# Nine row gathers move from GpSimd to single-row loads on SyncE and ScalarE, in a recurrent scoring kernel

## The chip, the core and the metric

The kernel runs on one core of a Trainium2 chip. The metric is the device time of one execution in microseconds. Three runs before the change gave 1564.42, 1565.53 and 1565.64 us; the median is 1565.53 us. Engines are named as the profile names them: PE is TensorE, DVE is VectorE, ACT is ScalarE, POOL is GpSimd, SP is SyncE.

## What is computed

A batch of 1024 sequences of 50 item numbers looks up a table of 100001 rows of 128 floats. The running mean of the rows is normalised over the batch, drives a neuron that spikes, and the mean spike count of each sequence is multiplied with the whole table.

```python
emb = emb_table.at[0].set(0.0)
e = emb[seq]                              # 1024 x 50 x 128
prefix = jnp.cumsum(e, axis=1)
uF = prefix / jnp.minimum(t_idx, lengths)
y = (uF - uF.mean(axis=0)) * lax.rsqrt(uF.var(axis=0) + BN_EPS) * gamma + beta
def step(v, x):                           # scanned over the 50 steps
    v = v + (x - v) / TAU
    spike = atan_spike(v - V_TH)
    return v - spike * V_TH, spike
scores = spikes.mean(axis=0) @ emb.T      # 1024 x 100001
```

The scores take 409.6 MB in HBM; they are the kernel's output.

## The kernel before

**Two stages.** The first runs the 50 steps. The second multiplies the counts with the table in 98 parts of 1024 rows (L498 to L578): PE multiplies (L161), DVE and ACT move the product from PSUM to SBUF (L553, L555), and SP issues the stores (L170). The table's first parts are loaded at the very start of the kernel (L110), over some 60 us.

**One step.** The batch is eight pieces of 128 sequences. For step t, `gather(t)` (L205) makes a tile `e` of 128 x 1024, and POOL issues one indirect load for each piece (L208). There are two buffers of `e`, so the gathers of step t+2 stand behind PE's last reading of the `e` of step t. PE turns the eight pieces one after the other into `pre` (L351), which keeps the running sum, in two halves of four. For each half DVE scales the sum into `uF` (L362) and takes statistics (L363). Then follow in turn: DVE's aggregate (L371), ACT's square root (L375) and centring of `uF` (L382), small steps on DVE (L388 to L401), ACT's `x` (L405), DVE's step that makes the new `v` (L408), and ACT's `over` (L321), which makes the tile `d` from `v`. `d` is used in the next step. `uF` has one buffer and `pre` is one sum, so two steps overlap little on PE, DVE and ACT; only the gathers run ahead, by two buffers.

**The single rows.** In six steps (`BY_SYNC`, L36) the eighth piece is not gathered. `fetch_singles` (L221) has SP load the byte addresses of 16 rows into registers (L226, a TENSOR_LOAD) and issue 16 loads of one row of 512 bytes (L229), eight times over. The 128 rows land in one of four slots of `held_rows`, and PE reads the slot as its eighth piece (L353). The first set is written into the program ahead of the steps, each further set in the step that uses up the set before. SP has nothing else to do in the first stage after the loads of the table.

**What holds a load back.** All loads and stores of SP and ACT take turns on eight counting semaphores, DMAHW0 to DMAHW7, in an order that is fixed when the program is built. A load adds 16 to its semaphore when its data has landed, and waits, on the engine that issues it, until the load before it on the same semaphore has landed. In the first stage before the change only SP issues such loads.

Of the kernel before, what the change touches and what calls it, by code (L numbers as in the profile page):

```python
# [17 lines left out]
U8 = mybir.dt.uint8  # L18
# [3 lines left out]
P = 128  # L22
# [4 lines left out]
BANK = 512  # L27
# [5 lines left out]
SHIFT = TWICE + ASIDE  # L33
FURTHER = {5: 1, 6: 2}

BY_SYNC = (12, 19, 26, 33, 40, 47)  # L36
AT_ONCE = 16

WIDTHS = 4 * [2] + 4 * [3] + 13 * [6]
NARROW, MIDDLE = 4, 8  # L40
# [3 lines left out]
def rec_kernel(  # L44
# [9 lines left out]
    nc = tc.nc  # L54
    B, T = seq.shape
    N, D = table.shape
    NB = B // P
# [16 lines left out]
    held_rows = const.tile([P, BANK], F32, tag="countB", name="held_rows")  # L74
# [13 lines left out]
    def pair(i):  # L88
        free.append([embp.tile([P, HALF], F32R, tag=f"{x}{i}", name=f"{x}_{i}") for x in ("hi", "lo")])
# [59 lines left out]
    def prepare(q, pt):  # L149
        turned(q, pt)  # L150
        split[q] = hi, lo = free.pop(0)
        vp, vh, vl = views(q, pt, hi, lo)
        nc.scalar.copy(vh, vp)  # L153
        nc.vector.tensor_tensor(vl, vp, vh.bitcast(F32), ALU.subtract)  # L154
# [18 lines left out]
    with ExitStack() as ph:  # L173
# [30 lines left out]

        def gather(t):  # L205
            es[t] = gp.tile([P, B], F32, tag="e", name=f"e_{t}")
            for n in range(NB - (t in BY_SYNC)):
                nc.gpsimd.indirect_dma_start(  # L208
                    out=es[t][:, n * P : (n + 1) * P],
                    out_offset=None,  # L210
                    in_=table,
                    in_offset=bass.IndirectOffsetOnAxis(ap=idx[:, n, t : t + 1].bitcast(U32), axis=0),
                )

        byte_rows = table.rearrange("n d -> (n d)").bitcast(U8)
        row_bytes = 4 * D
        starts = ids[:T, :P].bitcast(I32)
        regs = [nc.sync.alloc_register(f"row{k}") for k in range(AT_ONCE)]
        singles = {}

        def fetch_singles(i):  # L221
            t = BY_SYNC[i]
            rows_of = held_rows[:, i % (BANK // P) * P :][:, :P]
            singles[t] = rows_of
            for p0 in range(0, P, AT_ONCE):
                nc.sync.load(regs, starts[t : t + 1, p0 : p0 + AT_ONCE])  # L226
                for k, reg in enumerate(regs):
                    at = nc.sync.snap(reg, donate=True, min_val=0, max_val=(N - 1) * row_bytes)
                    nc.sync.dma_start(  # L229
                        out=rows_of[p0 + k : p0 + k + 1, :].bitcast(U8),  # L230
                        in_=byte_rows[bass.ds(at, row_bytes)].rearrange("(o b) -> o b", o=1),
                    )

        make_identity(nc, ident)
        isz = up.tile([P, NB, P], F32, tag="uF", name="isz")
        rb = up.tile([P, NB, P], F32, tag="uF", name="rb")
        gather(0)

        last_ids = ids[:, P : P + T]
        nc.vector.tensor_copy(last_ids, idx[:, NB - 1, :])  # L240
        ips = vp.tile([P, B], F32, tag="v0", name="ips")
        nc.tensor.transpose(ips[:T, :P], last_ids, ident)
        nc.vector.tensor_scalar_mul(starts, ips[:T, :P], float(row_bytes))
        fetch_singles(0)

        nc.vector.memset(isz, 0.0)
# [47 lines left out]
        def only(t):  # L294

            k = t % ONLY
            if k == 0:
                n = min(ONLY, T - t)
                nc.vector.tensor_tensor(
                    ls[:, :n, :],  # L300
                    r0n.unsqueeze(1).to_broadcast([P, n, D]),
                    sel[:, t : t + n].unsqueeze(2).to_broadcast([P, n, D]),
                    ALU.mult,
                )
            return ls[:, k, :]
# [12 lines left out]
        def over(t, v):  # L318

            d = lp.tile([P, B], BF16, tag="d", name=f"d_{t}")  # L320
            nc.scalar.activation(d, v, AF.Identity, bias=less)  # L321
            return d
# [4 lines left out]
        def spiked(out, cs, v):  # L327
            nc.vector.scalar_tensor_tensor(out, v, V_TH, count[:, cs], ALU.is_ge, ALU.add)
# [12 lines left out]
        correct(0, only(0))  # L341
        l = only(1)
        gather(1)
        for t in range(T):
            last = t == T - 1
# [18 lines left out]
            if t + 2 < T:  # L364
                gather(t + 2)
            if t in BY_SYNC[:-1]:
                fetch_singles(BY_SYNC.index(t) + 1)
            if not last:
# [35 lines left out]
            def x(vt, cs):  # L404
                nc.scalar.activation(vt, uF[:, cs], AF.Identity, bias=hgb[:, 1:2], scale=a)  # L405

            def step(vt, cs):
                nc.vector.scalar_tensor_tensor(vt, negv[:, cs], -0.5, vt, ALU.mult, ALU.add)  # L408

            if not last:  # L410
                vt = vp.tile([P, B], F32, tag=f"v{(t + 1) % 2}", name=f"v_{t}")
                x(vt, whole)
                if t:
                    spiked(count, whole, v)
                step(vt, whole)
                v = vt
                if t == T - 2:
                    spiked(count, whole, v)
                    moved = once.tile([P, P], F32, tag="r0hi", name="moved")
                    nc.vector.tensor_scalar_add(moved, v[:, pieceA], beta2)  # L420
                    near = once.tile([P, P], F32, tag="r0", name="near")
                    nc.vector.scalar_tensor_tensor(near, v[:, pieceA], V_TH, moved, ALU.is_ge, ALU.subtract)
                d = over(t, v)
                if t + 2 < T:
                    l = only(t + 2)

                if t in (T - 8, T - 6):
                    q = (t - T + 8) // 2
                    pair(q)
                    prepare(q, vp.tile([P, HALF], F32, tag="v0", name=f"pt_{q}"))  # L430
                    if q == TWICE - 1:
                        for k in range(TWICE):
                            rows[GROUP + ASIDE + k] = first[:, k, :]
                        nc.sync.dma_start(
                            out=first[:, :TWICE, :],
                            in_=table[(GROUP + ASIDE) * HALF : (GROUP + SHIFT) * HALF, :].rearrange(
                                "(q p k) d -> p q (k d)", p=P, k=KQ
                            ),
                        )
# [58 lines left out]
    for c, W in enumerate(WIDTHS):  # L498
# [38 lines left out]
        for n, q in blockwise:  # L537
# [4 lines left out]
            o = os[n]  # L542
# [27 lines left out]
            if n in (1, 4) and c >= MIDDLE and to_fetch < parts:  # L570
                g, k = divmod(to_fetch - SHIFT, GROUP)
# [26 lines left out]
```

## Time and profile before

| | |
|---|---|
| median of three runs (lowest, highest) | 1565.53 us (1564.42, 1565.64) |
| profiled execution: its time, its span | 1564.15 us, 1562.4 us |
| first stage: first gather, last gather issued | 3.54 us, 496.29 us |
| first store of scores issued | 504.70 us |
| busy over the span: PE, DVE, ACT, POOL | 1118.9, 948.1, 673.4, 374.5 us |
| written to HBM | 409.60 MB |

The profile is one execution. Times in it count from the start of the span. Time is cut by engine, and each group of instructions has its line in the kernel, the tile it writes and reads, the count, the busy time and the idle time ahead of it with what ended that. Rows marked SPq or ACTq are loads issued by SP or ACT.

### The profile page before, as it was taken

What the parts mean: (1) busy time and instruction counts of PE and PEld (TensorE: products, weight loads), DVE (VectorE), ACT (ScalarE), POOL (GpSimd) and SP (SyncE); (2) the same over time, 40 slices, a digit from 0 to 9 for tenths busy, and PEclk for the clock granted to TensorE, in tenths of its full rate; (3) what the DMA queues carried; (4) which work ended last, traced back from release to release, by engine and by line L of the source; (5) the groups of instructions that cost most, each with busy time, mean ns of one, the idle gap of its engine ahead of it and who ended that gap; (6) DMA issues with size and microseconds to landing.
All of it is one profiled execution on the core that took longest, in us unless ns stands there. A gap on an engine that the chain in (4) does not pass through costs nothing.

```text
span 1562.4 us, 13860 instructions
## 1 busy us (share of the span) xinstructions
PE 1118.9 (72%) x4465; PEld 794.4 (51%) x4465; DVE 948.1 (61%) x1128; ACT 673.4 (43%) x698; POOL 374.5 (24%) x400
## 2 busy tenths in 40 slices
PE   4444444444445989989888888888877888877883
PEld 2212111111123767667666666666666666666663
DVE  5777677777778655667555555555555455555552
ACT  2333333333334545555444444444444444444442
POOL 7777777777775000000000000000000000000000
PEclk9999999999999999999999999999999899999998
DMA  9722222222222999999999999999999999999997
GB/s 347 269 54 54 55 55 54 54 55 54 52 80 62 402 411 416 421 414 396 431 422 429 433 425 406 432 424 432 416 425 421 402 428 425 429 422 418 430 409 338
DMA packets 52813, 488.22 MB, mean 312 GB/s; under 512 B 10767, under 2 KB 11792, under 8 KB 31620
## 3 DMA queue, kind: packets, MB, share of 16 engines
q1 hardware_dynamic: 32432, 431.26, 65.7%
q0 software_dynamic: 12608, 25.85, 6.3%
q10 hardware_dynamic: 7700, 30.23, 4.7%
q8 instruction: 35, 0.57, 0.1%
q14 instruction: 38, 0.31, 0.1%
HBM read 77.69 MB, written 409.60 MB: 312 GB/s over the span
## 4 chain that ended last, share of the span: by engine, by line
DMA 47%; POOL 19%; PE 13%; issue 10%; DVE 5%; ACT 4%; ACTq 0%; POOLq 0%; SPq 0%; DVEq 0%
DMA scores<-o 45%; POOL e L208 19%; PE po L161 13%; DVE o L553 3%; ACT o L555 3%; DMA e<-in_L_rec_emb_table,idx 3%; DVE pairs L154 1%; ACT pairs L153 0%; PE pt L137 0%; PE pre L351 0%; ACT hi L153 0%; PE warm L337 0%; DMA idx<-in_r_seq 0%; DVE lo L154 0%; ACTq L555 0%
## 5 line engine op out<-in xcount | busy, mean ns | idle before, releaser
L553 DVE TENSOR_SCALAR o<-po 128x1024 f32<-128x1024 f32 (+1 forms) x390 | 465.5, 1213 | 326.2 <-DMA scores<-o 192.1
L555 ACT ACTIVATE o<-po 128x1024 f32<-128x1024 f32 x392 | 392.6, 1026 | 498.4 <-DMA scores<-o 377.8
L208 POOL DMA_INDIRECT e<-in_L_rec_emb_table,idx x394 | 373.8, 949 | 122.1 <-issue 117.1
L161 PE MATMUL po<-pairs,countB 128*128 128x512 f32 (+1 forms) x1120 | 293.3, 408 | 65.3 <-ACT o L555 65.3
L351 PE MATMUL pre<-ident,e 128*128 128x128 f32 x394 | 174.9, 463 | 220.7 <-DMA e<-in_L_rec_emb_table,idx 220.1
L161 PEld LDWEIGHTS po<-pairs,countB 128*128 128x128 f32 x1120 | 211.1, 194 | 127.7 <-ACT o L555 85.2
L161 PE MATMUL po<-pairs,countC 128*128 128x512 f32 (+1 forms) x840 | 230.9, 421 | 57.5 <-ACT o L555 49.0
L351 PEld LDWEIGHTS pre<-ident,e 128*128 128x128 f32 x394 | 72.5, 185 | 326.1 <-DMA e<-in_L_rec_emb_table,idx 325.2
L161 PEld LDWEIGHTS po<-pairs,countC 128*128 128x128 f32 x840 | 162.2, 200 | 107.0 <-ACT o L555 60.7
L154 DVE TENSOR_TENSOR pairs<-pt,pairs 128x1024 fp32r<-128x1024 f32 x70 | 85.3, 1218 | 95.3 <-ACT pairs L153 95.2
L362 DVE SCALAR_TENSOR_TENSOR uF<-rlen,pre 128x512 f32<-128x512 f32 x100 | 68.3, 683 | 100.0 <-PE pre L351 100.0
L137 PE MATMUL pt<-ident,rows 128*128 128x128 f32 (+1 forms) x768 | 107.1, 286 | 10.4 <-DVE rows L134 4.9
L137 PEld LDWEIGHTS pt<-ident,rows 128*128 128x128 f32 (+1 forms) x768 | 96.5, 149 | 28.0 <-issue 11.7
L375 ACT ACTIVATE r<-mv,eps 128x1 f32<-128x1 f32 x50 | 14.8, 295 | 212.2 <-DVE mv L371 212.2
L161 PE MATMUL po<-hi,countB 128*128 128x512 f32 x208 | 85.1, 409 | 13.4 <-ACT o L555 11.9
L309 PE MATMUL pre<-zT,ls 128*128 128x512 f32 x100 | 78.1, 783 | 21.9 <-DVE uF L362 18.0
L153 ACT CAST pairs<-pt 128x1024 fp32r<-128x1024 f32 x70 | 70.1, 1014 | 42.1 <-PE pt L137 42.1
L161 PE MATMUL po<-lo,countB 128*128 128x512 f32 x208 | 83.0, 399 | 0.0
L321 ACT ACTIVATE d<-v,less 128x1024 bf16<-128x1024 f32 x49 | 54.6, 1114 | 65.4 <-DVE v L408 62.2
L161 PE MATMUL po<-hi,countC 128*128 128x512 f32 x156 | 67.1, 430 | 14.7 <-ACT o L555 12.9
L405 ACT ACTIVATE v<-uF,hgb,a 128x1024 f32<-128x1024 f32 x49 | 59.2, 1208 | 30.6 <-DVE a L401 30.5
L161 PE MATMUL po<-pairs,countA 128*128 128x512 f32 x280 | 68.9, 393 | 3.7 <-ACT o L555 3.0
(94 smaller groups left out, 855.1 us busy)
## 6 DMA issues: line engine op xcount, KB each, us to landing
scores<-o SPq DMA_DIRECT2D x96, 3072.0 KB
scores<-o SPq DMA_DIRECT2D x32, 1536.0 KB
scores<-o SPq DMA_DIRECT2D x29, 1024.0 KB
rows<-in_L_rec_emb_table ACTq DMA_DIRECT2D x19, 1536.0 KB
scores<-o SPq DMA_DIRECT2D x8, 2896.5 KB
rows<-in_L_rec_emb_table SPq DMA_DIRECT2D x5, 3072.0 KB
held_rows<-in_L_rec_emb_table SPq DMA_DIRECT2D x768, 0.5 KB
e<-in_L_rec_emb_table,idx POOLq DMA_INDIRECT x394, 2.5
```

The lines of the kernel that those rows point to most:

```text
L137: nc.tensor.transpose(pt[:, k0 : k0 + pw], r[:pw, k0 : k0 + D], ident[:pw, :pw])
L153: nc.scalar.copy(vh, vp)
L154: nc.vector.tensor_tensor(vl, vp, vh.bitcast(F32), ALU.subtract)
L161: nc.tensor.matmul(po[:, :kw], lhsT=counts[n], rhs=part[:, k0 : k0 + kw], start=j == 0, stop=j == 1,)
L208: nc.gpsimd.indirect_dma_start(out=es[t][:, n * P : (n + 1) * P], out_offset=None, in_=table, in_offset=bass.IndirectOffsetOnAxis(ap=idx[: ...
L309: nc.tensor.matmul(pre[h], lhsT=l, rhs=zT[:, h * BANK : (h + 1) * BANK], start=t == 0, stop=False, skip_group_check=True,)
L321: nc.scalar.activation(d, v, AF.Identity, bias=less)
L351: nc.tensor.matmul(pre[h][:, k : k + P], lhsT=singles[t] if h * BANK + k + P == B and t in singles else e[:, h * BANK + k : h * BANK + k + P],
L362: nc.vector.scalar_tensor_tensor(uF[:, cs], rlen[:, cs], 1.0 / (t + 1), pre[h], ALU.max, ALU.mult)
L405: nc.scalar.activation(vt, uF[:, cs], AF.Identity, bias=hgb[:, 1:2], scale=a)
L553: nc.vector.tensor_scalar_mul(o[:, h0 : h0 + hw], po[:, :hw], 1.0 / T)
L555: nc.scalar.mul(o[:, h0 : h0 + hw], po[:, :hw], 1.0 / T)
```

## The change

`BY_SYNC` now names seven steps: 12, 17, 23, 29, 35, 40, 46 (before: 12, 19, 26, 33, 40, 47). `AT_ONCE` is 32, so SP takes 32 addresses in each TENSOR_LOAD, four per set. The sets of SP share two slots of `held_rows`, not four. Two further steps (`BY_SCALAR`: 25 and 41) get their eighth piece from ACT: in each step from 7 on, behind `over`, ACT loads 8 addresses and issues 8 row loads, so that a set takes 16 steps: 7 to 22 for step 25, and 23 to 38 for step 41. Each has a slot of its own. POOL thus issues 391 gathers, not 394; SP issues 896 single rows, not 768, and ACT 256.

```diff
-BY_SYNC = (12, 19, 26, 33, 40, 47)
-AT_ONCE = 16
+BY_SYNC = (12, 17, 23, 29, 35, 40, 46)
+AT_ONCE = 32
+BY_SCALAR = (25, 41)
+SCALAR_FROM = 7
+SCALAR_ROWS = 8
...
-            for n in range(NB - (t in BY_SYNC)):
+            for n in range(NB - (t in BY_SYNC + BY_SCALAR)):
...
+        slots = [held_rows[:, k : k + P] for k in range(0, BANK, P)]
+        scalar_regs = [nc.scalar.alloc_register(f"own{k}") for k in range(SCALAR_ROWS)]
+
+        def fetch_rows(engine, some, t, p0):
+            n = min(len(some), P - p0)
+            engine.load(some[:n], starts[t : t + 1, p0 : p0 + n])
+            for k, reg in enumerate(some[:n]):
+                at = engine.snap(reg, donate=True, min_val=0, max_val=(N - 1) * row_bytes)
+                engine.dma_start(
+                    out=singles[t][p0 + k : p0 + k + 1, :].bitcast(U8),
+                    in_=byte_rows[bass.ds(at, row_bytes)].rearrange("(o b) -> o b", o=1),
+                )
+
         def fetch_singles(i):
             t = BY_SYNC[i]
-            rows_of = held_rows[:, i % (BANK // P) * P :][:, :P]
-            singles[t] = rows_of
+            singles[t] = slots[i % 2]
             for p0 in range(0, P, AT_ONCE):
...
+                fetch_rows(nc.sync, regs, t, p0)
+
+        scalar_todo = [(t, p0) for t in BY_SCALAR for p0 in range(0, P, SCALAR_ROWS)]
+
+        def fetch_some():
+            t, p0 = scalar_todo.pop(0)
+            singles[t] = slots[2 + BY_SCALAR.index(t) % 2]
+            fetch_rows(nc.scalar, scalar_regs, t, p0)
...
                 d = over(t, v)
+                if t >= SCALAR_FROM and scalar_todo:
+                    fetch_some()
```

The built program differs in more than the counts. The first place is SP in its first set, for step 12. Before, each row names the next of the eight semaphores, 4, 5, 6, 7, 0, 1, and so on; every load on them is SP's.

```order
L229 DMA held_rows<-in_L_rec_emb_table 1x512 [waits DMAHW4_49]
L226 TENSOR_LOAD ids
L229 DMA held_rows<-in_L_rec_emb_table 1x512 [waits DMAHW5_49]
L229 DMA held_rows<-in_L_rec_emb_table 1x512 [waits DMAHW6_49]
L229 DMA held_rows<-in_L_rec_emb_table 1x512 [waits DMAHW7_49]
L229 DMA held_rows<-in_L_rec_emb_table 1x512 [waits DMAHW0_49]
L229 DMA held_rows<-in_L_rec_emb_table 1x512 [waits DMAHW1_49]
L229 DMA held_rows<-in_L_rec_emb_table 1x512 [waits DMAHW2_49]
L229 DMA held_rows<-in_L_rec_emb_table 1x512 [waits DMAHW3_49]
```

Now the same engine, from its 32nd row on (the row ahead of the second TENSOR_LOAD), in the changed kernel, where L229 is the load of addresses and L232 the row:

```order
L232 DMA held_rows<-in_L_rec_emb_table 1x512 [waits DMAHW4_49]
L229 TENSOR_LOAD ids
L232 DMA held_rows<-in_L_rec_emb_table 1x512 [waits DMAHW5_49]
L232 DMA held_rows<-in_L_rec_emb_table 1x512 [waits DMAHW6_49]
L232 DMA held_rows<-in_L_rec_emb_table 1x512 [waits DMAHW7_49]
L232 DMA held_rows<-in_L_rec_emb_table 1x512 [waits DMAHW0_49]
L232 DMA held_rows<-in_L_rec_emb_table 1x512 [waits DMAHW1_49]
L232 DMA held_rows<-in_L_rec_emb_table 1x512 [waits DMAHW3_49]
L232 DMA held_rows<-in_L_rec_emb_table 1x512 [waits DMAHW5_49]
L232 DMA held_rows<-in_L_rec_emb_table 1x512 [waits DMAHW7_49]
```

From its 38th row on SP names only every second semaphore: the turns between are ACT's. The second place is ACT in step 7. Before, `over` is followed at once by the square root of the next step:

```order
L321 ACTIVATE d_678<-v_674,less 128x1024 [waits DVE_49]
L375 ACTIVATE r_707<-mv_705,eps 128x1 [waits DVE_49]
L382 ACTIVATE uF_680<-uF_680,mv_705 128x1024 [waits Activation_49]
L405 ACTIVATE v_717<-uF_680,hgb,a_713 128x1024 [waits DVE_49,Activation_49]
L321 ACTIVATE d_721<-v_717,less 128x1024 [waits DVE_49]
```

Now (L337 is `over`, L391 the square root) the load of addresses and eight rows stand between them:

```order
L337 ACTIVATE d_674<-v_670,less 128x1024 [waits DVE_49]
L229 TENSOR_LOAD ids [waits DVE_49]
L232 DMA held_rows<-in_L_rec_emb_table 1x512 [waits DMAHW5_49]
L232 DMA held_rows<-in_L_rec_emb_table 1x512 [waits DMAHW6_49]
L232 DMA held_rows<-in_L_rec_emb_table 1x512 [waits DMAHW7_49]
L232 DMA held_rows<-in_L_rec_emb_table 1x512 [waits DMAHW0_49]
L232 DMA held_rows<-in_L_rec_emb_table 1x512 [waits DMAHW1_49]
L232 DMA held_rows<-in_L_rec_emb_table 1x512 [waits DMAHW2_49]
L232 DMA held_rows<-in_L_rec_emb_table 1x512 [waits DMAHW3_49]
L232 DMA held_rows<-in_L_rec_emb_table 1x512 [waits DMAHW4_49]
L391 ACTIVATE r_712<-mv_710,eps 128x1 [waits DVE_49]
```

ACT's rows take their turns in the middle of SP's set. In the built program each wait names a count as well. SP's 33rd row waits until DMAHW5 stands at 96, which is six loads of 16; the sixth load on DMAHW5 is the first row of ACT's step 7. Going through all counts gives the rows of SP that wait for a row of ACT. In the table, rows are numbered 1 to 128 in their set, and ACT's rows 1 to 8 in their step.

| SP's set, for step | the steps of ACT that its rows wait for | the last such step: SP row <- ACT row |
|---|---|---|
| 12 | 7, 8, 9, 10, 11 | step 11: 96 <- 5, 98 <- 6, 100 <- 7, 102 <- 8 |
| 17 | 12, 13, 14, 16 | step 16: 68 <- 1, 72 <- 5, 74 <- 6, 76 <- 7, 78 <- 8 |
| 23 | 17, 18, 19, 21, 22 | step 22: 94 <- 5, 96 <- 6, 98 <- 7, 100 <- 8 |
| 29 | 23, 24, 25, 27, 28 | step 28: as for 23 |
| 35 | 29, 30, 31, 33, 34 | step 34: as for 23 |
| 40 | 35, 36, 37, 38 | step 38: 66 <- 5, 68 <- 6, 70 <- 7, 72 <- 8 |
| 46 | none | none |

ACT's rows wait for rows of SP in the same manner, but for earlier ones: those of step 16 wait for row 61 of the set for 17, those of step 22 for rows 78 to 84 of the set for 23.

More of the change, by code (lines that the diff above doesn't have):

```diff
@@ L219, in rec_kernel @@
         singles = {}
+        slots = [held_rows[:, k : k + P] for k in range(0, BANK, P)]
[9 more added lines that the diff above has]
+                )
         def fetch_singles(i):
             t = BY_SYNC[i]
-            rows_of = held_rows[:, i % (BANK // P) * P :][:, :P]
-            singles[t] = rows_of
+            singles[t] = slots[i % 2]
             for p0 in range(0, P, AT_ONCE):
[L226 to L232, printed above, removed]
+                fetch_rows(nc.sync, regs, t, p0)
[4 more added lines that the diff above has]
+            fetch_rows(nc.scalar, scalar_regs, t, p0)
         make_identity(nc, ident)
```

## The prediction

> **What bounds the kernel now.** I read the page first, then busy time in windows, then the waits of SP, then single steps in the timeline. The page's slices (39 us each) show two stages.
>
> ```profile
> span 1562.4 us, 13860 instructions
> POOL 7777777777775000000000000000000000000000
> DMA  9722222222222999999999999999999999999997
> L208 POOL DMA_INDIRECT e<-in_L_rec_emb_table,idx x394 | 373.8, 949 | 122.1 <-issue 117.1
> L351 PE MATMUL pre<-ident,e 128*128 128x128 f32 x394 | 174.9, 463 | 220.7 <-DMA e<-in_L_rec_emb_table,idx 220.1
> ```
>
> In the first stage POOL is busy in every slice and the DMA engines hardly; POOL waits for next to nothing but its own issue (117.1 of 122.1 us idle), so a gather takes (373.8 + 117.1) / 394 = 1.25 us. PE waits 220 us for them. So POOL paces the steps: eight gathers, 10.0 us. Two windows (length, busy time with counts of PE, PEld, DVE, ACT and POOL, then PEclk, DMA share, GB/s) show the stages apart:
>
> ```profile
> 200.00:300.00 100.00, 48.16 (x103) 19.40 (x103) 74.31 (x125) 37.85 (x42) 75.60 (x81) 1.00 0.22 55
> 600.00:1562.00 962.00, 789.88 (x3500) 619.31 (x3498) 521.17 (x440) 433.78 (x438) 0.00 (x0) 0.95 0.99 418
> ```
>
> The second stage has the DMA engines 99% busy with stores. It cannot shrink or stretch for anything done here, so every microsecond by which the first stage ends earlier or later reaches the end. Of 100 us in the first stage DVE, the busiest behind POOL, works 74.31. The time from one `over` (L321) to the next is my measure of a step:
>
> ```profile
> 132.66 1.11 ACT L321 ACTIVATE d<-v,less 128x1024 bf16<-128x1024 f32 x1 [1.30 <-DVE v L408]
> ...
> 201.34 0.82 DVE L299 TENSOR_TENSOR ls<-r0n,sel 128x640 fp32r<-128x640 f32 x1
> 201.46 1.11 ACT L321 ACTIVATE d<-v,less 128x1024 bf16<-128x1024 f32 x1 [1.29 <-DVE v L408]
> 203.79 0.45 PE L351 MATMUL pre<-ident,held_rows 128*128 128x128 f32 x1
> 210.45 1.12 ACT L321 ACTIVATE d<-v,less 128x1024 bf16<-128x1024 f32 x1 [1.30 <-DVE v L408]
> ...
> 416.86 1.11 ACT L321 ACTIVATE d<-v,less 128x1024 bf16<-128x1024 f32 x1 [1.30 <-DVE v L408]
> 436.36 1.11 ACT L321 ACTIVATE d<-v,less 128x1024 bf16<-128x1024 f32 x1 [1.30 <-DVE v L408]
> 448.28 1.11 ACT L321 ACTIVATE d<-v,less 128x1024 bf16<-128x1024 f32 x1 [1.30 <-DVE v L408]
> 456.45 1.11 ACT L321 ACTIVATE d<-v,less 128x1024 bf16<-128x1024 f32 x1 [1.30 <-DVE v L408]
> 469.21 1.11 ACT L321 ACTIVATE d<-v,less 128x1024 bf16<-128x1024 f32 x1 [1.30 <-DVE v L408]
> 472.42 0.30 ACT L375 ACTIVATE r<-mv,eps 128x1 f32<-128x1 f32 x1 [2.09 <-DVE mv L371]
> 476.90 1.11 ACT L321 ACTIVATE d<-v,less 128x1024 bf16<-128x1024 f32 x1 [1.30 <-DVE v L408]
> ...
> 501.01 0.29 ACT L375 ACTIVATE r<-mv,eps 128x1 f32<-128x1 f32 x1 [2.52 <-DVE mv L371]
> ```
>
> These are steps 11, 18, 19, 40, 42, 43, 44, 45 and 46, and the square roots of 46 and of the last step, 49. Step 19 shows the path behind a single-row piece: turned at 203.79, `over` at 210.45, so 6.7 us. Steps 43 and 45 take 11.9 and 12.8 us (the table parts prepared there), and step 46, whose gathers lay ready, 7.7 us: the pace of the chain when POOL isn't waited for.
>
> **What the change gives.** Not nine gathers go, but three: six had gone already. 3 x 1.25 = 3.75 us, if POOL stays the bound.
>
> **What it costs: SP waits for ACT.** The rows of SP and ACT share eight semaphores, and a row waits on its engine for the load before it on its semaphore. That such a wait stops SP shows in SP's waits:
>
> ```profile
> SPq L229 <- DMA rows<-in_L_rec_emb_table: 14.8, 2, 8.7
> ```
>
> Two rows stood up to 8.7 us until the table's loads, their predecessors, had landed. Beyond these, rows wait for earlier rows, unseen, as SP runs ahead of need: each set was whole long before its step. In the changed program SP can't run ahead: row 96 of the set for step 12 waits for ACT's fifth row of step 11, and this load is issued only behind `over` of step 11. The eighth piece of step 12 is due 2.3 us behind that `over` (201.46 to 203.79). The rest of the set is issued in that time and later. Its length comes from these rows:
>
> ```profile
> L226 SPq TENSOR_LOAD <-ids x48: 1200/1256/1426, 39.3 to 374.6; - x48
> L229 SPq DMA_DIRECT2D held_rows<-in_L_rec_emb_table x481: 227/228/283, 99.9 to 299.7; - x161
> e<-in_L_rec_emb_table,idx POOLq DMA_INDIRECT x394, 2.5
> L110 ACTq DMA_DIRECT2D rows<-in_L_rec_emb_table x19: 374/374/432, 793.6 to 1398.9; - x19
> 1102.11 1.03 ACT L555 ACTIVATE o<-po 128x1024 f32<-128x1024 f32 x1 [0.37 <-PE po L161]
> 1102.11 0.37 ACTq L110 DMA_DIRECT2D rows<-in_L_rec_emb_table  x1
> ```
>
> - A row on SP: (299.7 - 99.9) / 480 = 0.416 us with its share of the load, 1.26 / 16 = 0.08: 0.33 us. On ACT I take the same; ACT's own load is 0.374 us plus the gap of some 0.1 us between SP's (0.33 - 0.23), so 0.47 us is the upper end.
> - A load of 32 addresses: no row. Between one load of 16 (1.26, nothing per register) and two (2.5). I take 1.9. A load of 8, likewise, 0.63 to 1.26: 0.95.
> - Landing of a row: not shown. A gather lands 2.5 us from its issue, 0.95 of that on POOL: 1.55 us. Rows 0.33 us apart on eight semaphores never waited for each other, so under 2.6 us; above the 0.23 us of the issue. I take 1.5.
> - ACT issued a load in the same 10 ns as an ACTIVATE began (1102.11): the sequencer goes on while the engine computes. So ACT's batch starts with `over`, at T: the load ends at T + 1.0, row 5 is issued at T + 2.4 and lands at T + 3.9, row 8 is issued at T + 3.4.
>
> From these, how long a step with a late set takes (SP still has to load 32 addresses ahead of row 97):
>
> - Step 12: SP's row 96 goes at T + 3.9; then 0.33 + 1.9 + 31 x 0.33 = 12.5; landed 1.5 later, T + 17.9; plus 6.7: **24.6 us**.
> - Step 17: row 72 waits for ACT's row 5 of step 16: 25 rows, load, 31 rows = 20.4; T + 3.9 + 20.4 + 1.5 + 6.7 = **32.5**.
> - Steps 23, 29, 35: row 94: 3 rows, load, 31 rows = 13.1: **25.2** each.
> - Step 40: row 66 waits for step 38; 31 rows, load, 31 rows = 22.3: **34.4** for steps 39 and 40 together.
>
> Sum 167.1 us for 7 steps. The earlier gates of a set are passed while the steps go on, since between them stand some 25 rows, 8 us. ACT's rows wait for SP's only in rows issued a step before: nothing.
>
> The other 22 steps from 12 to 40 run at the chain's pace. 7.7 us, plus 0.82 / 5 for the step in five that has L299, plus ACT's batch: it ends at T + 3.65, the square root is due at T + 3.2 (469.21 to 472.42): 0.45. Together 8.3 us; 22 x 8.3 = 182.6. The gathers keep up: at a late set POOL has filled both buffers and stopped; it goes on once the next step's tile is read, at the latest at that `over`, and lands its eight pieces 12.6 us later, two and a half steps ahead of their use; it loses 1.7 us a step on the chain and isn't met again before the next set.
>
> So `over` of step 40 comes 167.1 + 182.6 = 349.7 us behind that of step 11, against 416.86 - 132.66 = 284.2: 65.5 us late. Then some comes back: before, POOL paced the rest, 501.01 - 416.86 = 84.2 us; now the 55 gathers left need 55 x 1.25 = 68.7 and the chain paces it: 6 x 7.7 + 11.9 + 12.8 + 3.2 = 74.1. Net 65.5 - 10.1 = **+55.4 us**; the 3.75 us of POOL are in this, as POOL no longer counts.
>
> The set for step 46 waits for nobody: begun when 40's has landed, 128 x 0.33 + 4 x 1.9 = 50 us, whole at `over` 40 + 45, due at + 50. The two slots cost nothing: a slot is read one set before it is refilled. The 512-byte rows don't load the DMA engines (22% busy). On SP only stores stand behind, later still.
>
> The profiled execution took 1564.15 us, 1.75 over its span and 1.4 below the median. 1564.15 + 55.4 = **1620 us**.
>
> The loads of addresses are the place for a rule. Measured: 16 registers in 1.26 us, 79 ns each at most. The Trainium skill (Runtime: NRT & Kernel Launch, section on instruction fetch mechanics) puts a register load at about 200 ns per register, even in bulk; that is 3.2 us for 16, so this trace doesn't bear it out. By that rule loads of 32 and 8 would take 6.4 and 1.6 us, and the sum would be 4.5 x 6 + 0.65 x 28 = 45 us higher, 1665 us.
>
> **The rivals.**
>
> 1. *The buffers hide it, and it is faster.* While a set is late, gathers go on into two buffers, and each step at the chain's pace wins 10.0 - 8.3 = 1.7 us back. That decides at 5 x 1.7 = 8.5 us of lateness per set of six steps: below it POOL paces the stage still and 3 gathers are gained, 1564.15 - 3.75 = 1560.4 us. I count 25.2 - 8.7 = 16.5 us. It takes 24 rows less behind the gate. For it: before, POOL never stopped for the 12 us steps. Against: the counts of rows. 5%.
> 2. *ACT's batch is dearer:* it starts at the end of `over` (+1.1 us), or its rows cost 0.47 us (8 x 0.14 = 1.1). The square root waits 1.1 us longer in 22 steps and the gates open up to 1.1 us later in 6 sets: +31 us, 1651 us; both, 1682. For it: the one row of ACT's own loads. Against: 1102.11. 17%.
> 3. *Loads of addresses grow faster than their registers*, as the square: 4 x 1.26 = 5.0 us for 32, and 1.26 for 8. In 6 late sets and 28 batches of ACT on the path (22 steps, 6 gates) that is 3.1 x 6 + 0.31 x 28 = +27 us, 1647 us. For it: no row of 32. Against: 1.26 us for 16 leaves little per register. 4%. The rule of the skill's Runtime page is a case of it.
> 4. *ACT's batch is fully covered and rows land in 1 us:* 22 x 0.45 and 2 x 0.5 x 6 less: 1604 us. Inside the range.
>
> **How the numbers follow.** 74% for the forecast with rival 4, 17, 4 and 5% for the others. The low end takes rival 4 and a load of 32 at 1.26 us (6 x 0.64 less): 1600. The high end takes rival 2 with the load at 2.5 us and some of its second half: 1668. A measurement of this kernel tells 0.2%, about 3 us. Slower 0.94: all but rival 1. Faster 0.04, same 0.02: rival 1 with its gain of 3.75 us whole or partly lost.
>
> **What would show it.** SP's rows waiting for ACT's rows in SP's waits, some tens of us in all; PE waiting for `held_rows` in six steps, up to 20 us each; POOL idle until PE's `pre` (L351's new line), 55 to 60 us in all, where all its idle time but issue was 5 us; about 8 us between the other `over`s, not 10; the second stage the same length. I am wrong if sets are whole before their step, if POOL's idle time ends on issue alone, or if the steps between take 10 us.

## The result and the profile after

Four runs of the changed kernel gave 1613.16 to 1614.21 us, median 1614.02; four of the kernel before gave 1564.37 to 1565.64, median 1564.97. The ratio is 1.0315, with a 95% interval of 1.0302 to 1.0328: the change makes the kernel 49 us slower. The profiled execution took 1613.16 us with a span of 1611.4 us, 49.0 us more than before.

First lines of the page of the changed kernel, as they were shown for the kernel before, and then the two windows (the first the same, the second to the new end):

```profile
span 1611.4 us, 14644 instructions
POOL 7777746767657300000000000000000000000000
L211 POOL DMA_INDIRECT e<-in_L_rec_emb_table,idx x391 | 371.4, 950 | 171.9 <-issue 111.1
...
L367 PE MATMUL pre<-ident,held_rows 128*128 128x128 f32 x9 | 4.0, 442 | 134.2 <-DMA held_rows<-in_L_rec_emb_table 134.2
```

```profile
200.00:300.00 100.00, 30.39 (x91) 19.78 (x91) 61.09 (x107) 30.64 (x35) 58.02 (x62) 0.50 0.17 43
600.00:1611.00 1011.00, 840.10 (x3705) 658.89 (x3703) 553.25 (x466) 460.40 (x464) 0.00 (x0) 0.94 0.99 417
```

POOL now has gaps (digits 4 to 6 among the 7s) and works into a fourteenth slice. In 100 us of the first stage it issues 62 gathers, not 81, and no engine is fuller for it: DVE works 61, not 74 us. Something else paces the steps, and the idle time of PE ahead of the nine `held_rows` pieces, 134.2 us, names it. The second stage is as before, 99% DMA at 417 GB/s. The waits of the first stage (total us, times, longest), of SP, PE and POOL in the changed kernel:

```profile
SPq L232 <- DMA held_rows<-in_L_rec_emb_table: 99.5, 43, 18.7
PE pre L367 <- DMA held_rows<-in_L_rec_emb_table: 134.2, 7, 29.4
POOL e L211 <- PE pre L367: 55.3, 15, 15.5
```

Before, SP waited for no row of `held_rows`, PE for none either, and POOL waited for PE 1.5 us in all. Now SP's rows wait 99.5 us for other rows; PE waits for the set; and POOL, with both buffers of `e` full, waits for PE. The timeline of step 17 (start, duration, then what ended the wait ahead) has the three in a row, with the `over`s of steps 11, 12, 38 and 40 around it and that of step 48 at the end:

```profile
132.65 1.11 ACT L337 ACTIVATE d<-v,less 128x1024 bf16<-128x1024 f32 x1 [1.30 <-DVE v L424]
157.38 1.11 ACT L337 ACTIVATE d<-v,less 128x1024 bf16<-128x1024 f32 x1 [1.30 <-DVE v L424]
...
188.37 1.11 ACT L337 ACTIVATE d<-v,less 128x1024 bf16<-128x1024 f32 x1 [1.30 <-DVE v L424]
189.23 2.71 ACTq L232 DMA_DIRECT2D held_rows<-in_L_rec_emb_table  x8
202.18 0.94 POOL L211 DMA_INDIRECT e<-in_L_rec_emb_table,idx  x1 [0.30 <-issue]
214.66 0.45 PE L367 MATMUL pre<-ident,held_rows 128*128 128x128 f32 x1 [29.43 <-DMA held_rows<-in_L_rec_emb_table]
218.66 0.94 POOL L211 DMA_INDIRECT e<-in_L_rec_emb_table,idx  x1 [15.54 <-PE pre L367]
221.31 1.11 ACT L337 ACTIVATE d<-v,less 128x1024 bf16<-128x1024 f32 x1 [1.30 <-DVE v L424]
...
440.89 1.11 ACT L337 ACTIVATE d<-v,less 128x1024 bf16<-128x1024 f32 x1 [1.30 <-DVE v L424]
477.33 1.11 ACT L337 ACTIVATE d<-v,less 128x1024 bf16<-128x1024 f32 x1 [1.30 <-DVE v L424]
...
546.58 1.11 ACT L337 ACTIVATE d<-v,less 128x1024 bf16<-128x1024 f32 x1 [3.14 <-DVE near L438]
```

`over` of step 16 is at 188.37, and ACT's eight rows stand right behind it. The last row of SP's set has landed 26.3 us after that `over`, when PE turns the set at 214.66; POOL stopped at 203.1, and `over` of step 17 is 32.94 us behind that of step 16. From `over` 11 to `over` 40 the stage takes 344.7 us, where it took 284.2: 60.5 us late. From `over` 40 to `over` 48 it takes 69.25 us; before it took 80.5 (416.86 to 497.37): 11.3 us come back. 60.5 - 11.3 = 49.2 us, the whole difference.

### The profile page after: what moved, and what is told of

The parts are those of the page before. It is cut to its first block, busy times and chain, and to the rows that moved or that the text cites. A ratio compares the mean times of both kernels' runs of the same rounds, so it can differ in the third digit from the quotient of the medians.

```text
span 1611.4 us, 14644 instructions
## 1 busy us (share of the span) xinstructions
PE 1080.5 (67%) x4465; PEld 809.4 (50%) x4465; DVE 947.7 (59%) x1128; ACT 674.3 (42%) x698; POOL 372.1 (23%) x397
## 4 chain that ended last, share of the span: by engine, by line
DMA 45%; PE 16%; DVE 13%; ACT 9%; SPq 6%; issue 5%; POOL 4%; ACTq 1%; DVEq 0%; POOLq 0%
DMA scores<-o 40%; PE po L164 15%; SPq L232 5%; POOL e L211 4%; DVE o L571 3%; DVE v L424 3%; ACT o L573 3%; ACT v L421 3%; DMA held_rows<-in_L_rec_emb_table 3%; DVE bs L379 2%; DMA e<-in_L_rec_emb_table,idx 2%; DVE uF L378 1%; DVE negv L341 1%; ACTq L232 1%; ACT uF L398 1%
## 5 line engine op out<-in xcount | busy, mean ns | idle before, releaser
L164 PE MATMUL po<-pairs,countC 128*128 128x512 f32 (+1 forms) x840 | 239.7, 433 | 58.7 <-ACT o L573 52.0
L164 PEld LDWEIGHTS po<-pairs,countC 128*128 128x128 f32 x840 | 167.8, 207 | 111.0 <-ACT o L573 64.0
L367 PE MATMUL pre<-ident,e 128*128 128x128 f32 x391 | 118.2, 432 | 66.3 <-DMA e<-in_L_rec_emb_table,idx 66.1
L367 PEld LDWEIGHTS pre<-ident,e 128*128 128x128 f32 x391 | 78.5, 209 | 105.8 <-DMA e<-in_L_rec_emb_table,idx 99.3
L391 ACT ACTIVATE r<-mv,eps 128x1 f32<-128x1 f32 x50 | 14.8, 295 | 273.1 <-DVE mv L387 160.8
L325 PEld LDWEIGHTS pre<-zT,ls 128*128 128x128 f32 x100 | 29.9, 300 | 172.0 <-DVE uF L378 167.7
L140 PE MATMUL pt<-ident,rows 128*128 128x128 f32 (+1 forms) x768 | 105.8, 283 | 10.1 <-DVE rows L137 4.9
L164 PE MATMUL po<-hi,countB 128*128 128x512 f32 x208 | 85.2, 410 | 13.6 <-ACT o L573 12.0
L367 PE MATMUL pre<-ident,held_rows 128*128 128x128 f32 x9 | 4.0, 442 | 134.2 <-DMA held_rows<-in_L_rec_emb_table 134.2
L337 ACT ACTIVATE d<-v,less 128x1024 bf16<-128x1024 f32 x49 | 54.6, 1114 | 65.4 <-DVE v L424 62.3
L164 PE MATMUL po<-hi,countC 128*128 128x512 f32 x156 | 67.7, 434 | 13.6 <-ACT o L573 12.4
```

The source lines that it names most:

```text
L140: nc.tensor.transpose(pt[:, k0 : k0 + pw], r[:pw, k0 : k0 + D], ident[:pw, :pw])
L164: nc.tensor.matmul(po[:, :kw], lhsT=counts[n], rhs=part[:, k0 : k0 + kw], start=j == 0, stop=j == 1,)
L325: nc.tensor.matmul(pre[h], lhsT=l, rhs=zT[:, h * BANK : (h + 1) * BANK], start=t == 0, stop=False, skip_group_check=True,)
L367: nc.tensor.matmul(pre[h][:, k : k + P], lhsT=singles[t] if h * BANK + k + P == B and t in singles else e[:, h * BANK + k : h * BANK + k + P],
```

## The experiments

Eight kernels were timed in twelve runs, four of them twice. Each run's ratio is to the kernel before on the same chip. Seven of the twelve runs were on a chip on which the kernel before itself took 1780 us, not 1565; five were where it took 1564. What follows rests on those five; the seven are told last.

Theory: rows of SP wait for rows of ACT, which are issued one batch a step; the rows of a set that stand behind such a gate come too late, and the step waits. Rivals: the seven sets with 32 addresses a load and two slots are too slow by themselves; ACT's batch lengthens the steps; SP's waits are harmless and something else stops PE.

**SP's part alone** (e5).

```diff
-BY_SCALAR = (25, 41)
+BY_SCALAR = ()
```

> SP's part alone once more: in e1 the kernel before itself took 1780 us, and in stretches each instruction of SP took 0.7 us in place of 0.03 to 0.23, so e1 says nothing of the waits. Where the kernel before takes about 1565 us: theory (SP's rows wait for ACT's; here there are none): POOL paces the steps and one gather is gained, 1565 - 1.25 = 1563.7 us. Rival (SP itself is too slow with closer sets, longer loads and two slots): over 1595 us.

Measured: 1563.53 us (11 runs, 1563.28 to 1563.93), ratio 0.9994, interval 0.9985 to 1.0003. Of this kernel, the window that was shown of the other two, and then the waits of SP and POOL:

```profile
200.00:300.00 100.00, 48.23 (x103) 19.37 (x102) 73.07 (x125) 37.46 (x41) 75.61 (x81) 0.50 0.21 54
```

```profile
SPq L232 <- DMA rows<-in_L_rec_emb_table: 15.0, 2, 9.0
POOL e L211 <- issue: 115.9, 380, 0.3
```

The 15.0 us are those that the kernel before had, for the loads of the table. SP's waits for `held_rows` are gone, and POOL waits for its own issue; 81 gathers fit into 100 us again. SP alone carries seven sets with four loads of 32 addresses and two slots, and PE waits for a set once, 0.9 us. So the whole loss comes with ACT's two sets; whether by the gate or by the batch's own time, this run doesn't say.

**ACT's part with the sets as they were** (e6): SP keeps its old steps (six sets, seven steps apart) and its old loads, on two slots; ACT's 32 batches stay.

```diff
-BY_SYNC = (12, 17, 23, 29, 35, 40, 46)
-AT_ONCE = 32
+BY_SYNC = (12, 19, 26, 33, 40, 47)
+AT_ONCE = 16
```

> ACT's part alone, as e2, where the kernel before takes about 1565 us. SP's rows wait for ACT's up to the step before each set's, but only 16 rows and one load of 16 stand behind row 112. Theory: sets 9 to 10 us late every seven steps; six steps at 7.8 in place of 10.0 us win 13 us back, so the buffers hide it: 392 gathers, -2.5 us, and 0 to 3 us more from the set of step 12: 1562.5 to 1565.5 us. Rival (ACT's loads and rows themselves lengthen the steps): 1590 us or more. Rival (any wait for ACT costs its lateness in full): 1580 us or more.

Measured: 1564.6 us (1563.75 to 1566.16), ratio 1.0002, interval 0.9993 to 1.0011. Its waits of SP, PE and POOL:

```profile
SPq L232 <- DMA held_rows<-in_L_rec_emb_table: 91.3, 58, 19.1
PE pre L367 <- DMA held_rows<-in_L_rec_emb_table: 65.4, 5, 16.6
POOL e L211 <- PE pre L367: 6.0, 12, 2.7
```

SP waits almost as long as in the change (91.3 against 99.5 us), sets come late (step 12 takes 25.7 us, steps 19, 26 and 33 take 20.6 to 21.3, step 40 18.5), and it costs nothing. POOL doesn't stop, 6.0 us in all: while a set is late its gathers run on into the buffers, and the steps between, 7.5 to 8.4 us long, use them up. A step with a single-row piece has seven gathers, 8.75 us. So per seven steps 21 - 8.75 = 12 us are lost and 6 x (10 - 7.8) = 13 won back. This is rival 1 of the prediction, in a kernel in which its condition holds, and it shows that SP's wait and ACT's 32 batches need not cost what they cost in the change. Nothing is gained either: 392 gathers are left, two fewer than before, and their 2.5 us are lost in POOL's 6.0. In the change a cycle has six steps and a set 26 us: 17 lost, 5 x (10 - 7.84) = 11 won back.

**The second set of ACT alone** (e7): ACT starts in step 23, so only the sets for 29, 35 and 40 meet it.

```diff
-BY_SCALAR = (25, 41)
-SCALAR_FROM = 7
+BY_SCALAR = (41,)
+SCALAR_FROM = 23
```

> The changed kernel with ACT's second set alone, as e4, where the kernel before takes about 1565 us. Theory: sets 12, 17 and 23 in time, step 29 takes 26 us, of which the buffers take most, 35 takes 26, 39 and 40 take 36, the steps between 7.8: 34 us late at step 40, of which 10 to 11 come back: 1565 + 23 = 1588 us. Rival (SP too slow by itself): late from step 17 on, near 1614 us. Rival (ACT's batches cost, in proportion to their number): half of 49 us as well, but late evenly from step 23 on, with no step over 12 us.

Measured: 1585.83 us (1585.44 to 1586.33), ratio 1.0138, interval 1.0123 to 1.0154. The waits of SP and POOL in this kernel:

```profile
SPq L232 <- DMA held_rows<-in_L_rec_emb_table: 72.0, 28, 29.7
POOL e L211 <- PE pre L367: 26.2, 11, 12.3
```

From step 7 to step 28 each `over` is 8.8 to 10.3 us behind the one before, and sets 12, 17 and 23 are in time. Then step 29 takes 25.8 us, step 35 25.9, and steps 39 and 40 36.6, the lengths that they have in the change (26.2, 26.0, 36.4). The loss goes where ACT's loads go.

**The same rows of ACT in fewer steps** (e8): 13 rows in each of 20 steps, none in the one to three steps ahead of a set's use, so that SP's last wait for ACT opens a step or more earlier. It leaves more rows of SP behind that gate, not fewer: the order of the semaphores in the trace puts the first row that waits for the last batch at 63 to 80 in the sets for 23, 29 and 35, where the change has 94, and at 38 in the set for 40, where it has 66.

```diff
-SCALAR_FROM = 7
-SCALAR_ROWS = 8
+SCALAR_IN = (7, 8, 9, 10, 12, 13, 14, 17, 18, 19, 23, 24, 25, 26, 29, 30, 31, 32, 35, 36)
+SCALAR_ROWS = 13
...
-                if t >= SCALAR_FROM and scalar_todo:
+                if t in SCALAR_IN and scalar_todo:
```

> The changed kernel with the same sets of SP and of ACT, 391 gathers and 256 rows on ACT, but ACT issues 13 rows in each of 20 steps and none in the last step, mostly the last two or three, ahead of a set of SP. So SP's last waits open a step or more earlier: step 10 for 12, 14 for 17, 19 for 23, 26 for 29, 32 for 35, 36 for 40. Theory: the sets are late by less, some still by over the 8 us that the buffers win back: +15 to +25 us, about 1585 us. Rival (ACT's work itself): a batch is now 13 rows long, so not under 1614 us.

Measured: 1611.24 us (1610.61 to 1611.58), ratio 1.0299, interval 1.0283 to 1.0315: the expectation missed by 26 us. Steps 17, 23, 29 and 35 do get shorter, 20.1, 16.1, 15.2 and 14.5 us, not 33 and 26; steps 39 and 40 still take 32.0, and SP's waits for rows are 98.0 us in all, as in the change. The batches got longer than expected. ACT's loads of addresses, those of steps 12 and 13 and all 20 (count, lowest/median/highest ns, start), and then the timeline of ACT with the batch of step 12 and the square root behind it:

```profile
L229 ACTq TENSOR_LOAD <-ids x1: 1231/1231/1231, 152.6 to 152.6; - x1
...
L229 ACTq TENSOR_LOAD <-ids x1: 3113/3113/3113, 162.9 to 162.9; - x1
...
L229 ACTq TENSOR_LOAD <-ids x20: 1202/3016/3113, 92.8 to 425.7; - x20
```

```profile
152.59 1.11 ACT L337 ACTIVATE d<-v,less 128x1024 bf16<-128x1024 f32 x1 [1.30 <-DVE v L424]
153.96 4.98 ACTq L232 DMA_DIRECT2D held_rows<-in_L_rec_emb_table  x13
158.99 0.29 ACT L391 ACTIVATE r<-mv,eps 128x1 f32<-128x1 f32 x1 [5.28 <-DMA held_rows<-in_L_rec_emb_table]
```

Even with the 1.2 us load the batch ends 6.4 us behind `over`, where the square root is otherwise due at about 3; with the 3.1 us load, two more. The steps that follow a batch take 9.7 to 12.5 us: hardly any wins anything back, so sets only 14 to 20 us long are not hidden either. Fourteen of the 20 loads are slow; 14 x 1.8 = 25 us is close to the miss. That is a sum and no test; loads that start at such whole multiples in the same steps were not tried.

**Nine sets off POOL, spaced by their gates** (e9): SP keeps its six old steps with 32 addresses a load, ACT brings three sets in batches of 12 rows in nearly every step, and none in steps 10 and 11. As in the change, 391 gathers are left.

```diff
-BY_SYNC = (12, 17, 23, 29, 35, 40, 46)
+BY_SYNC = (12, 19, 26, 33, 40, 47)
-BY_SCALAR = (25, 41)
-SCALAR_FROM = 7
-SCALAR_ROWS = 8
+BY_SCALAR = (22, 36, 48)
+SCALAR_IN = (7, 8, 9, 12, 13, 14, 15, 16, 17, 18, 19, 20, 21, 22, 23, 24, 25, 26, 27, 28, 29, 30, 31, 32, 33, 34, 35, 36, 37, 38, 39, 40, 41, 42, 43, 44, 45, 46, 47)
+SCALAR_ROWS = 12
...
-                if t >= SCALAR_FROM and scalar_todo:
+                if t in SCALAR_IN and scalar_todo:
```

> Nine sets leave POOL as in the change, 391 gathers, but SP has the six of before (every seven steps) in loads of 32, and ACT three: for steps 22, 36 and 48, 12 rows a step from 7 to 47, without steps 10 and 11. SP's rows still wait for ACT's up to the step before each set's, with 10 to 17 rows and at most one load of 32 behind the last wait. Theory: late by some 8 us every seven steps, and the steps between win that back though ACT's batch is longer: POOL paces the stage, 3 gathers gained, 1565 - 3.75 = 1561.3 us, faster than before. Rival (waits for ACT or its batches cost by themselves): slower than before, with 50% more rows on ACT at least 1600 us.

Measured: 1562.04 us (11 runs, 1561.09 to 1562.82), ratio 0.9985, interval 0.9976 to 0.9994: 2.2 us under the kernel before, below the 0.2% that a measurement surely tells, with an interval that leaves out 1. Its waits of SP, PE and POOL:

```profile
SPq L232 <- DMA held_rows<-in_L_rec_emb_table: 96.4, 93, 21.0
PE pre L367 <- DMA held_rows<-in_L_rec_emb_table: 19.3, 5, 6.1
POOL e L211 <- PE pre L367: 1.8, 6, 0.3
```

SP waits 96.4 us, as in the change, but PE waits 19.3 us, not 134.2, POOL 1.8, not 55.3. POOL is the bound again, and about 2.2 of its three gathers' 3.75 us arrive. So nine sets can leave POOL at a small gain. This kernel differs from the change in two ways at once: few rows stand behind a set's last gate, and SP has six sets to fetch, not seven.

**What the five runs say together.** Up to the set for step 40 SP only loads addresses, issues rows and waits, so each microsecond of waiting puts off all its later rows. The rows of that set in e5, in the change and in e9 (count, lowest/median/highest ns, first and last start):

```profile
L232 SPq DMA_DIRECT2D held_rows<-in_L_rec_emb_table x128: 227/228/345, 320.4 to 369.1; - x128
...
L232 SPq DMA_DIRECT2D held_rows<-in_L_rec_emb_table x128: 227/228/280, 411.5 to 469.0; - x128
...
L232 SPq DMA_DIRECT2D held_rows<-in_L_rec_emb_table x128: 227/228/263, 345.0 to 410.6; - x128
```

In e5 the last row starts at 369.1. `over` of step 40 can follow 8.3 us behind (469.0 to 477.33 in the change) and came at 415.5, so SP was 38 us ahead of need. In the change the row starts 99.9 us later, which is SP's 99.5 us of waits; 38 are covered, and `over` 40 comes 62 us behind that of e5. The same seven sets stand in e7 and e8: with waits of 72.0 and 98.0 us `over` 40 comes 34 and 60 us behind that of e5. In e6 and e9 SP has one set less to fetch up to step 40, some 51 us of its time, and would be 80 to 90 us ahead without waits (in e5 its fifth set is issued at 318). That covers most of their 91.3 and 96.4 us; e6 is 11 us late at `over` 40 and makes it up behind it. So the price of the waits is what exceeds SP's lead, less what the steps behind win back. Whether seven sets would go free with few rows behind each last gate is not shown: no run has both.

**The seven runs on the other chip.** There SP issues slowly in stretches. The timeline of SP in e1, the same kernel as e5:

```profile
205.58 13.57 SPq L232 DMA_DIRECT2D held_rows<-in_L_rec_emb_table  x7
```

Seven rows in 13.6 us, where a row takes 0.33 us otherwise. ACT issues slowly there too: in e12 one stretch of seven of its rows takes 7.56 us. Kernels with seven or eight sets of SP are slower there than the kernel before, those without any are faster, so these runs can't weigh a gate. What makes the issue slow on that chip was not found. The times that their expectations name take a kernel before of 1564 to 1570 us for granted and can't be held against them.

e1 is e5's kernel, e2 is e6's, e4 is e7's:

> Only SP's part of the change: seven sets, 32 addresses per load, two slots; ACT issues no rows, and steps 25 and 41 are gathered by POOL in full. Theory (SP's rows wait for ACT's): no row of SP has a predecessor on ACT, SP runs ahead, POOL paces the steps and one gather is gained, 1564.97 - 1.25 = 1563.7 us. Rival (SP itself is too slow with sets five or six steps apart, longer loads and two slots): sets still land late, most of the 49 us stay, over 1595 us.

> Only ACT's part: SP has the six sets and loads of 16 of before (on two slots), ACT issues the same 256 rows in the same 32 steps. SP's rows wait for ACT's here too, up to the step before each set's, but with only 16 rows and one load of 16 behind row 112. Theory: a set is 9 to 10 us late, every seven steps; six steps at 7.8 us in place of 10.0 win 13 us back, so the buffers hide it: 392 gathers, 1564.97 - 2.5 + 0 to 3 = 1562.5 to 1565.5 us. Rival (ACT's loads and rows themselves lengthen the steps): 32 steps over 10 us, 1590 us or more. Rival (any wait for ACT costs what it did): about +16 us for six sets less the 13: over 1580 us.

> The changed kernel with one of ACT's two sets: step 41's, issued from step 23 on; step 25 is gathered by POOL. SP's sets for 12, 17 and 23 then wait for nobody, those for 29, 35 and 40 wait for ACT as in the changed kernel. Theory: step 29 takes 26 us, of which the buffers take most; 35 takes 26, and 39 and 40 take 36; steps between take 7.8. That gives 16 - 10 + 16 - 6 + 18 = 34 us late at step 40, of which 10 to 11 come back: 1564.97 + 23 = 1588 us. Rival (SP too slow by itself): late from step 17 on as in the changed kernel, near 1614 us.

e3 takes away SP's sets, so that 398 gathers are left, and e12 is the same kernel again:

```diff
-BY_SYNC = (12, 17, 23, 29, 35, 40, 46)
+BY_SYNC = ()
...
-        fetch_singles(0)
+        if BY_SYNC:
+            fetch_singles(0)
```

> ACT's batches without any set of SP: POOL gathers all pieces but those of steps 25 and 41, 398 gathers. Theory: ACT's load and eight rows fit beside a step that POOL paces at 10.0 us, so only the gathers count: 1564.97 + 4 x 1.25 = 1570.0 us. Rival (ACT's batch is what costs): the 32 steps with a batch go over 10 us, 1590 us or more.

> ACT's batches with no set of SP, as e3, where the kernel before takes about 1564 us: 398 gathers. Theory: ACT's load and eight rows fit beside a step that POOL paces, so 1564.2 + 4 x 1.25 = 1569.2 us. Rival (ACT's batch costs by itself): 1590 us or more.

e10 is e8 with 16 rows in each of the steps 7, 8, 9, 12, 13, 14, 17, 18, 23, 24, 25, 29, 30, 31, 35 and 36; e11 has eight sets of SP, for steps 11, 16, 22, 27, 32, 38, 43 and 48, in four slots, and none of ACT:

> As e8, but in batches of 16 rows in 16 steps (7, 8, 9, 12, 13, 14, 17, 18, 23, 24, 25, 29, 30, 31, 35, 36): in e8 a load of 13 addresses took 3.0 us on ACT, where one of 8 takes 0.73 and one of 12 in e9 0.98, so e8's steps with a batch took 11 to 12 us. A load of 16 took 1.26 us on SP. The sets of SP and of ACT and the 391 gathers are those of the change; SP's last waits for ACT stand at step 9 for 12, 14 for 17, 18 for 23, 25 for 29, 31 for 35, 36 for 40. Theory: what costs is how late SP's waits open, so this is far under the change's +49 us: a batch takes 6.4 us and a step with one about 10.8, the sets are a few us late, +8 to +20 us, about 1578 us. Rival (ACT's work itself): longer batches, not under 1614 us.

> SP alone fetches eight sets, for steps 11, 16, 22, 27, 32, 38, 43 and 48, in loads of 32 and four slots; ACT none. No row of SP has a predecessor on ACT. A set takes 128 x 0.33 + 4 x 2.2 = 51 us, from about 110 us on, and is due every 5.3 steps of 9.8 us, 52 us. Theory: SP keeps up, 392 gathers, 1564.2 - 2.5 = 1561.7 us. Rival (SP is too slow for more than seven): late sets from step 32 on, 1570 us or more.

| run | us | kernel before there | ratio and interval |
|---|---|---|---|
| e1, SP's sets alone | 1821.53 | 1780.44 | 1.0255 (1.0204 to 1.0305) |
| e2, old sets of SP with ACT's | 1763.68 | 1780.44 | 0.9918 (0.9888 to 0.9947) |
| e3, ACT's sets alone | 1642.59 | 1780.44 | 0.9233 (0.9181 to 0.9286) |
| e4, ACT's second set | 1812.9 | 1780.44 | 1.0183 (1.0124 to 1.0241) |
| e10, 16 rows in 16 steps | 1798.98 | 1781.61 | 1.0104 (1.0051 to 1.0156) |
| e11, eight sets of SP | 1852.61 | 1781.61 | 1.0398 (1.0357 to 1.044) |
| e12, ACT's sets alone | 1643.12 | 1781.61 | 0.922 (0.9173 to 0.9268) |

Without any row of SP, and with four gathers more than before, the kernel is 8% faster there: on that chip SP's rows cost the kernel before most of its extra time. They are not all of it, as without them it still takes 1643 us, 74 more than e12's expectation. e5 to e7 repeat e1, e2 and e4 where this is not so; the same kernel has the ratio 1.0255 as e1 and 0.9994 as e5. ACT's sets alone, 16 rows in 16 steps, and eight sets of SP were not timed where the kernel before takes 1564 us; their worth there stays open.

## Why the prediction was right

The prediction said 1620 us; 1614 is within its range. Its mechanism is the one seen: SP's rows wait for ACT's, sets come late, PE waits for them and POOL for PE. One step of it is not, the place in a set where SP stops. Step by step:

- **The bound and the second stage: as said.** 49.2 us of delay at `over` 48 stand against 49.0 us in the span.
- **SP waits for ACT: as said, and shown** by e5 (no ACT rows, no wait, no loss) and e7 (loss from the first set that meets ACT's rows).
- **Where SP stops: not as said.** The prediction let the earlier gates of a set pass and put the wait at the last one, row 94 or 66. SP's waits in the set for step 29 of the changed kernel, from 281 to 322 us (rows 1 to 71) and from 322 to 345 us (the rest):

```profile
SPq L232 <- DMA held_rows<-in_L_rec_emb_table: 12.7, 5, 4.7
...
SPq L232 <- DMA held_rows<-in_L_rec_emb_table: 1.1, 3, 0.6
```

  SP stops ahead of rows 16, 44 and 68, 3 to 5 us each, since between these gates ACT takes two steps, 15.7 us, and SP's own work only some 10 to 11. So it comes to row 94 about when that gate opens and stops there 0.8, 0.2 and 0.0 us in the sets for steps 23, 29 and 35. Row 94 goes 4.2 to 4.4 us behind `over`, not 3.9. In the set for step 40 SP comes to row 66 after the gate has opened, and that row goes 5.4 us behind `over` (446.29 against 440.89). The step of the prediction that failed cost the sum little, because the last gate opens at nearly the time at which SP arrives.
- **The late sets: 172.3 us for seven steps, 167.1 predicted.** Step 12 took 24.7 (24.6), 17 took 32.9 (32.5), 23, 29 and 35 took 26.0 to 26.2 (25.2), 39 and 40 together 36.4 (34.4). About half of the 5.2 us is the later passing of the last gate, 1.7 the load of 32 addresses, 2.18 us, not 1.9, in six sets, and the rest the way from a set's last row to `over`, 8.3 to 8.5 us, not 8.2. ACT's part was a little cheaper than taken: a load of 8 took 0.73 us, not 0.95, and the batch of step 16 ended at 191.94, 3.57 us behind `over`, not 3.65. The changed kernel's loads and rows:

```profile
L229 ACTq TENSOR_LOAD <-ids x32: 723/732/756, 92.8 to 440.9; - x32
L229 SPq TENSOR_LOAD <-ids x28: 2116/2176/2375, 39.2 to 508.1; - x28
...
L232 ACTq DMA_DIRECT2D held_rows<-in_L_rec_emb_table x256: 217/217/520, 93.7 to 444.7; - x128
```

- **The other 22 steps: 172.4 us, 182.6 predicted.** This is the largest error: 10.2 us too many here, 5.2 too few in the late sets, and 1.2 too few that come back make the 6 us. A step took 7.84 us, not 8.3, because its base of 7.7 was too long. It was read from step 46 of the kernel before, and I took its gathers to lie ready. They did not. The first row is PE's wait in that step of the kernel before; the second is the square root in step 47 of the changed kernel, whose `over` 46 was at 530.04:

```profile
470.22 0.47 PE L351 MATMUL pre<-ident,e 128*128 128x128 f32 x1 [0.88 <-DMA e<-in_L_rec_emb_table,idx]
```

```profile
530.04 1.11 ACT L337 ACTIVATE d<-v,less 128x1024 bf16<-128x1024 f32 x1 [1.30 <-DVE v L424]
532.91 0.29 ACT L391 ACTIVATE r<-mv,eps 128x1 f32<-128x1 f32 x1 [1.76 <-DVE mv L387]
```

  PE still waited 0.88 us for a gather in step 46, and the square root came 3.21 us behind `over`; with all gathers there it comes after 2.87, and the step takes 7.35 us (steps 41, 42, 46 and 47 after the change). So the chain's pace was 0.35 us shorter than the one that I took for it. The steps with ACT's batch run at 7.4 to 8.2 us, so the batch and L299 together cost 0.49 on average, where the prediction had 0.61.
- **What comes back: 11.3 us, 10.1 predicted.** This is not the faster chain: the six plain steps took 46.7 us, 46.2 predicted, as step 48 took 9.2. Step 45 took 10.7, not 12.8.
- **No cost for the set of step 46, the slots, the 512-byte rows: as said**; steps 46 and 47 are as short as any, and e5 runs with the two slots and seven sets at no loss.
- **Rival 1 (the buffers hide it)** did not happen in the change, but it is real: e6 and e9 are it. Its point of decision was put at 8.5 us lost per six steps; with 7.84 us a step it is 11. The change loses 17.
- **Rival 2 (ACT's batch dearer)** fell: 189.23 shows the first row issued while `over`, begun at 188.37, still ran for 0.25 us, so its load of 0.73 us began with `over`. The eight rows took 2.71 us, 0.34 each, not 0.47.
- **Rival 3 (loads of addresses grow as the square)** fell: 0.73 us for 8, 1.26 for 16, 2.18 for 32 is linear. The Trainium skill (Runtime: NRT & Kernel Launch, section on instruction fetch mechanics) gives about 200 ns per register, in a passage on the register loads that the runtime puts in; for these loads from SBUF it doesn't hold: 2.18 / 32 = 68 ns.
- **Rival 4 (batch covered, landing in 1 us)** fell: its 1604 is 10 us off, the forecast 6. The batch is nearly covered (it ends 3.57 us behind `over`, and the square root is due at 2.87). But a row lands in 1.5 us or more, and the prediction took 1.5: the first row of ACT's step 27, and SP's row 68 that waits on the same semaphore, 1.48 us later:

```profile
319.12 0.45 ACTq L232 DMA_DIRECT2D held_rows<-in_L_rec_emb_table  x1
...
320.60 0.23 SPq L232 DMA_DIRECT2D held_rows<-in_L_rec_emb_table  x1
```

- **The signs: as said, but one.** POOL waited 55.3 us for PE where 55 to 60 were named; PE's longest wait for a set was 29.4 us, where up to 20 were named.

## What to carry to other kernels

Before giving loads to a second engine, see which counters they share with the first: a queue that ran far ahead is then tied to the pace of the other. Weigh its waits against its lead, that is, how far ahead of need it would be without them: 99.5 us of waits cost 49 us with 38 us of lead (11 came back), and 96.4 us cost nothing with 80 to 90. Then weigh a late load per cycle against what the steps between win back with the buffers there are: in these runs 12 us lost in seven steps cost nothing, and 17 lost in six left the excess in the time. Take the pace of a chain only from a step in which no engine shows a wait for the thing that paced it before.

## What the runs showed of the hardware

- **Loads of addresses into registers** took 0.73 us for 8, 0.98 for 12 (e9), 1.26 for 16 and 2.18 for 32, which fits 0.25 us and 0.245 us for every four. In e8, with 13 addresses of four bytes, the loads that start at the 1st, 53rd and 105th address of a set, whole multiples of 16 bytes, took 1.2 us, and those at other offsets 2.6 to 3.1, or 0.23 to 0.24 us for every single address. The offset and the time go together in all 20; why is not shown. Of the loads shown here the first starts 208 bytes into its set, the second 260.
- **The granted clock of TensorE** was 1.00 in the first stage before the change and 0.50 in the same window of e5, with the times of both within 0.1%: in a stage that POOL paces and in which PE is half idle it decided nothing.
- **A load of one 512-byte row** by ACT let the waiting row of SP go 1.48 us after its own issue began in one case (319.12 to 320.60) and 1.89 in another (263.26 to 265.15, the set for step 23).
- **On one chip** SP took 1.9 us a row in one stretch (13.57 / 7) and ACT 1.1 (7.56 / 7, e12), and the kernel before took 1780 us. A cause was not found.
